# A pool of their own for the exponents, head 0's key scales spread by GpSimd, and the first projection products placed among the attention's last ones

## The chip, the cores and the metric

The kernel runs on one core of one Trainium2 chip. The metric is the time of one execution on the device in microseconds; 2890.35 us is the median of three runs before the change (2888.08 to 2891.64). Five engines take part, each with its own queue of instructions that it works off in order: TensorE (PE), VectorE (DVE), ScalarE (ACT), GpSimd (POOL) and SyncE (SP). Transfers are issued from the queues of SP, POOL and ACT.

## The reference: what is computed

One layer of a perceiver: cross-attention of 512 tokens to 8192 context tokens, then causal self-attention, then a gated feed-forward block with four-bit weights. Each adds to `x`. The change lies in the cross-attention and in the step from it to the self-attention:

```python
q = (layernorm(x) @ Wq + bq)          # 512 x 1024, 16 heads of 64
kv = ctx @ Wkv + bkv                  # 8192 x 2048
q = fq_sym(q / 8, axis=-1)            # quantised to 127 steps, scale per token and head
k = fq_sym(k, axis=-1)                # the same, per key and head
v = fq_sym(v, axis=tokens)            # per column
attn = fq_unsigned(softmax(q @ k.T))  # 255 steps, scale per row
x = x + (attn @ v) @ Wp + bp          # "the projection"
x = x + self_attention(layernorm(x))  # causal, 4 sequences of 128, rotary
x = x + ffn(layernorm(x))             # silu(gate) * up, down, RMS norm
```

## The kernel before, in words

The work has five stages in program order.

1. The queries are computed, then values and keys of all 64 context tiles of 128 tokens (`project`, L336; `join`, L350). A float32 product is done as three products of rounded parts: a high part, a low part scaled up, and a difference (`split_hi` on ACT, `split_lo` on DVE). Keys are quantised (`quantise`), transposed by DMA (`transpose_k`, L565), cast on ACT into `kst` and stored to memory as `k_d` by POOL (`store_k`, L576). The keys' scales are collected for 16 tiles, transposed by TensorE, copied by ACT and stored as `sk_d` (`key_scales`, L595). There are four key chunks `c` of 2048 keys.
2. At the end of that stage, head 0's keys (`load_keys`, L611) and scales (`load_scales`, L620) are loaded on the SP queue. Each of the eight scale tiles `sk` is a DMA that writes one row of 1024 scales to all 128 partitions, 512 KB. For heads 1 to 15 four rows are loaded instead (`load_rows`, L731), and GpSimd broadcasts them over the partitions (`spread_scales`, L737).
3. Attention runs over 64 units (16 heads by 4 query tiles) of 8 steps each, 1024 keys a step. In the loop of L876, step `s` issues the scores of unit `s // 8` (`scores`, L746: two products into PSUM, then one DVE instruction at L766 that multiplies by the scales into `e` and takes the maximum), the exponentials of the unit before (`exponentials`, L789, ACT, 4096 wide, into int16 `a`), transposes of `a` with a lag of 12 steps (`transposes`, L803: by TensorE with an ACT copy of PSUM into `aT`; chunks 1 and 3 by DMA instead, `dma_transposes`, L817), and the products with the values with a lag of 18 steps (`values`, L828). After the last query tile of a head, DVE scales the result into `xo`. Since each queue is worked in order, the order of these calls is the order of work; 18 steps after the last scores only transposes and value products remain.
4. Projection and self-attention. A list of work (`do(step, function)`, L1198 on) is sorted by its step numbers and issued in that order. There are ten parts of 32 steps: part 0 and part 1 are the two halves of the projection by `Wp`. Part 0 uses whole float32 products (`first_step`, L1005) on transposed `xo` (`first_transposes`, L976, a TensorE transpose and ACT copies into `xoT`), so its weights `wp` need no splitting. Part 1 uses `product_step` (L1016), with the parts `x_h`, `x_l`, `x_d` of the input (`first_split`, L985) and `sw_h`, `sw_l`, `sw_d` of the weights. Weights come in pairs of rows, loaded on SP into `w_raw`, which has two buffers (`load_pair`, L953; `split_pair_hi`, `split_pair`). Each part has four pairs. The result is joined to `x1` by DVE (`join_residual`, L1038), after POOL has added the bias row (`add_row`, L973). PSUM accumulators have two buffers a tag.
5. The feed-forward block.

Memory is managed in pools that open and close as a stack on the left or the right side of SBUF. When a pool closes, the next one takes its bytes, and the first writer of the new tile waits for the last reader of the old one. In the kernel before, the exponents `e` are a tag of the pool `at` (L753), opened after `opool` and `at_s`.

Of the kernel before, what the change touches and what calls it, by code (L numbers as in the profile page):

```python
# [46 lines left out]
P = 128  # L47
# [15 lines left out]
LAG_V = NSC + 10  # L63
DMA_KC = (1, 3)
# [20 lines left out]
def tile_perceiver(  # L85
# [111 lines left out]
    nsq = qpool.tile([P, NT, H], F32, name="nsq")  # L197
# [113 lines left out]
    def double_q():  # L311
        nc.vector.tensor_scalar_mul(nsq, sq, -1.0)
        nc.scalar.dma_start(out=qT[D:P, 0:H:2, :], in_=qT[0:D, 0:H:2, :])
        nc.scalar.dma_start(out=qT[0:D, 1:H:2, :], in_=qT[D:P, 1:H:2, :])
# [280 lines left out]
    def key_scales(c):  # L595

        row = pools["k"].tile([P, 2 * P], F32, name="sk_row", tag="sk_row", bufs=1)
        for e in range(2):
            pt = kv_ps.tile([P, P], F32, name="sk_pt", tag="ps")
            nc.tensor.transpose(pt, sks[c].rearrange("p h (i e) -> p e h i", e=2)[:, e], ident)  # L600
            nc.scalar.copy(in_order(row, c)[:, :, e], pt)
# [18 lines left out]
    def load_scales(h, g):  # L620
        c, half = divmod(g, 2)
        nc.sync.dma_start(
            out=tile_of_scales(h, g), in_=sk_d[c][h, ts(half, SC)].partition_broadcast(P)
        )
# [78 lines left out]
    for c in range(NKC - 1):  # L703
        do(at + 0.3, load_keys, 0, c)
        for g in range(2 * c, 2 * c + 2):
            do(at + 0.3, load_scales, 0, g)
# [6 lines left out]
    opool_s = ExitStack()  # L713
    opool = opool_s.enter_context(tc.tile_pool(name="opool", bufs=1))
    xo = [opool.tile([P, NT, 512], F32, name=f"xo{n}", tag=f"x{n}") for n in range(2)]
    both = opool.tile([P, 2, C], F32, name="sv_bp", tag="x2")
    sv, bp = both[:, 0, :], both[:, 1, :]

    with tc.tile_pool(name="at_s", bufs=4) as small, tc.tile_pool(
        name="at", bufs=2  # L720
    ) as at, tc.tile_pool(name="sc_ps", bufs=2, space=PSUM) as sc_ps, tc.tile_pool(
        name="at_ps", bufs=3, space=PSUM
    ) as at_ps:
        vqs = {}
# [6 lines left out]
        def load_rows(h):  # L731

            sks_at[h] = at.tile([P, KC], F32, name=f"sk_row{h}", tag="sk_row", bufs=1)
# [12 lines left out]
        def scores(n, g):  # L746
# [5 lines left out]
            if g % (NSC // NEC) == 0:  # L752
                e = at.tile([P, EC], F32, name="e", tag="e", bufs=3)  # L753
                state[n]["e"].append(e)
# [22 lines left out]
        def maximum(n):  # L777
# [6 lines left out]
                m, m, nsq[:, t, h : h + 1], math.log(255.0), ALU.mult, ALU.add  # L784
# [4 lines left out]
        def exponentials(n, c):  # L789
# [9 lines left out]
                scale=sq[:, t, h : h + 1],  # L799
# [3 lines left out]
        def transposes(n, g):  # L803
# [9 lines left out]
            nc.scalar.copy(aT, pt.bitcast(I32))  # L813
# [48 lines left out]

        load_keys(0, NKC - 1)
        for g in range(NSC - 2, NSC):
            load_scales(0, g)
        load_rows(1)
        nc.sync.dma_start(out=sv, in_=sv_d[0].partition_broadcast(P))
        nc.sync.dma_start(out=bp, in_=xbp.partition_broadcast(P))
# [3 lines left out]
        def at_step(s):  # L872
            return divmod(s, NSC) if 0 <= s < n_steps else None

        with tc.manual_schedule():
            for s in range(n_steps + LAG_V):  # L876
# [25 lines left out]
                if at_step(s - LAG_V):  # L902
                    values(*at_step(s - LAG_V))

# [5 lines left out]
    xq.close()  # L910
    xpool = ctx.enter_context(tc.tile_pool(name="xpool", bufs=1, side="right"))
    x1 = xpool.tile([P, NT, C], F32, name="x1")
    sa_s = ExitStack()

    x3_s = ExitStack()
    x3pool = x3_s.enter_context(tc.tile_pool(name="x3pool", bufs=1, side="right"))
    x3 = [x3pool.tile([P, NT, NC, P], F32R, name=f"x3_{c}") for c in "hld"]
# [6 lines left out]
    sa_ps = sa_ps_s.enter_context(tc.tile_pool(name="sa_ps", bufs=2, space=PSUM))  # L924

# [8 lines left out]
    w_first = {}  # L934
    w3s = {}
    acc = {}
    live = {}

    def load_first(k):
        tag = "qT" if k < 4 else ("kT" if k < 6 else "aT")  # L940
        w = sa_f.tile([P, 512], F32, name=f"wp0_{k}", tag=tag, bufs=4 if k < 4 else 2)
        nc.sync.dma_start(out=w, in_=w_src2[0][:, k, :])
        w_first[k] = w

    def load_x(t):
        nc.sync.dma_start(out=x1[:, t, :], in_=x[ts(t, P), :])
# [37 lines left out]

    def first_split(t):  # L985
        hi, lo, df = (x[:, t] for x in x3)
        split(live["xoT", t], hi, lo, df)
        nc.scalar.mul(lo, lo, UP)
# [16 lines left out]
    def first_step(t, k):  # L1005
        if k == 0:
# [459 lines left out]
```

## Time and profile before

| What | Value |
|---|---|
| Median of three runs | 2890.35 us |
| The profiled execution | 2888.83 us |
| Its span, first to last instruction | 2887.1 us |
| Mean granted TensorE clock | 0.978 |
| PE busy | 2666.1 us (92%) |
| DVE busy | 2411.5 us (84%) |
| ACT busy | 1271.2 us (44%) |
| POOL busy | 444.4 us (15%) |
| Last product of stage 1 starts | 1499.10 us |
| First exponent `e` | 1510.93 us |
| Last `e` starts | 2149.31 us |
| Last product with the values | 2164.22 us, for 0.64 |
| First product of part 1 | 2208.82 us |

Times within the profile are counted from the first instruction. A row of a group gives the line, the engine, the operation, and out<-in by tile names; a bracket gives how long the engine stood idle before and what released it. The clock is the share of full speed that was granted to TensorE.

### The profile page before, as it was taken

The numbers are of one execution on the slowest core, as the hardware profiler recorded it, in microseconds if no ns is written. First come the engines' busy times: TensorE is split into PE (matmuls) and PEld (weight loads), VectorE is DVE, ScalarE is ACT, GpSimd is POOL, SyncE is SP. The second block draws the span as 40 slices with busy tenths as digits, with TensorE's granted clock in tenths as the row PEclk, the third lists the DMA queues.
The fourth block names the chain that finished last, engine by engine and source line by source line (L and its number), as shares of the span: only waits on it lengthen the run. The fifth ranks groups of instructions, "written<-read, shape, count | busy, mean of one in ns | idle before, by whom it ended". The sixth has DMA issues, their size and how long they took to land. (4 is left out here: it accounts for less than half of the span.)

```text
span 2887.1 us, 41022 instructions
## 1 busy us (share of the span) xinstructions
PE 2666.1 (92%) x15480; PEld 2066.9 (72%) x15480; DVE 2411.5 (84%) x3946; ACT 1271.2 (44%) x1409; POOL 444.4 (15%) x596
## 2 busy tenths in 40 slices
PE   8999999999999999999987777787778899799998
PEld 3788888888888888888864555555555777688876
DVE  6899999555799998889769999999986898676674
ACT  4211111111323333333218999999993245333332
POOL 0011111000012222222112233322311000000000
PEclk9999999999999999999998999999999999899999
DMA  5555565222447777777457788878773221122222
GB/s 186 173 195 203 193 214 206 94 98 93 135 133 199 199 183 193 183 193 184 109 154 145 153 164 168 164 162 154 155 132 121 95 70 63 54 92 93 94 90 93
DMA packets 454342, 417.33 MB, mean 145 GB/s; under 512 B 357184, under 2 KB 361856, under 8 KB 454144
## 3 DMA queue, kind: packets, MB, share of 16 engines
q1 hardware_dynamic: 407648, 260.58, 37.1%
q0 software_dynamic: 45440, 153.09, 16.6%
q8 instruction: 121, 1.98, 0.3%
q10 hardware_dynamic: 1056, 1.05, 0.2%
q14 instruction: 77, 0.63, 0.1%
HBM read 224.30 MB, written 104.34 MB: 114 GB/s over the span
## 5 line engine op out<-in xcount | busy, mean ns | idle before, releaser
L342 PE MATMUL kv_a<-w_h,c_h 128*128 128x512 f32 x2048 | 806.4, 394 | 0.0
L342 PE MATMUL kv_b<-w_d,c_d 128*128 128x512 f32 x2048 | 806.0, 394 | 0.3 <-DVE c_d L157 0.3
L342 PE MATMUL kv_a<-w_l,c_l 128*128 128x512 f32 x2048 | 806.0, 394 | 0.2 <-ACT w_l L245 0.2
L766 DVE CUSTOM_DVE_ANT_0 e<-sc,sk 128x1024 f32<-128x1024 f32 x512 | 593.2, 1219 | 16.2 <-DMA k_d<-kst 8.2
L794 ACT ACTIVATE a<-e,m,sq 128x4096 int16<-128x4096 f32 x128 | 487.0, 3805 | 25.0 <-DVE m L783 24.8
L342 PEld LDWEIGHTS kv_a<-w_l,c_l 128*128 128x128 f32 x2048 | 384.8, 188 | 89.6 <-ACT w_l L245 0.6
L342 PEld LDWEIGHTS kv_b<-w_d,c_d 128*128 128x128 f32 x2048 | 384.8, 188 | 89.5 <-DVE c_d L157 0.7
L342 PEld LDWEIGHTS kv_a<-w_h,c_h 128*128 128x128 f32 x2048 | 384.9, 188 | 88.9 <-issue 0.2
L153 ACT ACTIVATE c_h<-c_raw 128x1024 fp32r<-128x1024 f32 x128 | 135.2, 1057 | 414.7 <-PE kv_a L342 405.5
L356 DVE SCALAR_TENSOR_TENSOR f<-kv_a,bkv 128x512 f32<-128x512 f32 x256 | 175.8, 687 | 163.4 <-PE kv_a L342 162.8
L759 PE MATMUL sc<-kt,qT 64*128 64x512 bf16 x1024 | 207.3, 397 | 108.9 <-DVE mx L766 104.6
L581 ACT CAST kst<-kT 128x512 bf16<-128x512 int16 x128 | 89.4, 698 | 310.1 <-DMA kT<-ki 310.0
L809 PE MATMUL a_pt<-ident,a 128*128 128x128 f32 x1024 | 176.9, 298 | 22.7 <-ACT a L794 18.0
L357 DVE SCALAR_TENSOR_TENSOR f<-kv_b,f 128x512 f32<-128x512 f32 x256 | 176.7, 690 | 20.0 <-DVE f L356 1.4
L739 POOL PARTITION_BROADCAST sk<-sk_row x120 | 142.7, 1299 | 317.9 <-DVE mx L766 317.8
L809 PEld LDWEIGHTS a_pt<-ident,a 128*128 128x128 f32 x1024 | 112.9, 146 | 88.6 <-ACT a L794 50.6
L759 PEld LDWEIGHTS <-qT 64*128 64x128 bf16 x1024 | 74.8, 93 | 137.3 <-issue 107.8
L156 DVE TENSOR_TENSOR fw_l<-fw_raw,fw_h 128x1024 fp32r<-128x1024 f32 x64 | 78.3, 1223 | 107.1 <-ACT fw_h L153 107.0
L156 DVE TENSOR_TENSOR c_l<-c_raw,c_h 128x1024 fp32r<-128x1024 f32 x128 | 155.7, 1216 | 6.0 <-ACT c_h L153 5.5
L157 DVE SCALAR_TENSOR_TENSOR c_d<-c_l,c_raw 128x1024 fp32r<-128x1024 f32 x128 | 156.3, 1221 | 2.3
L153 ACT ACTIVATE fw_h<-fw_raw 128x1024 fp32r<-128x1024 f32 x64 | 67.7, 1060 | 179.5 <-PE y_a L1369 75.2
L548 ACT CAST vq<-vi 128x1024 f16<-128x1024 int16 x64 | 66.9, 1046 | 172.2 <-DVE vi L541 123.8
(189 smaller groups left out, 4100.6 us busy)
## 6 DMA issues: line engine op xcount, KB each, us to landing
c_raw<-in_ctxT SPq DMA_DIRECT2D x128, 512.0 KB, 3.8
v_d<-f POOLq DMA_DIRECT2D x64, 512.0 KB, 3.1
vl<-v_d POOLq DMA_DIRECT2D x64, 512.0 KB, 4.2
gu_d<-w_ffn POOLq DMA_DIRECT2D x44, 512.0 KB, 3.2
fw_raw<-gu_d SPq DMA_DIRECT2D x42, 512.0 KB, 3.2
k_d<-kst POOLq DMA_DIRECT2D x128, 128.0 KB, 3.6
vq_d<-vq POOLq DMA_DIRECT2D x32, 512.0 KB, 5.1
kt<-k_d SPq DMA_DIRECT2D x64, 256.0 KB, 3.5
```

The costliest lines, as they stand in the source:

```text
L153: nc.scalar.mul(hi, src, 1.0 - 0.5 / UP)
L156: nc.vector.tensor_tensor(lo, src, hi, ALU.subtract)
L157: nc.vector.scalar_tensor_tensor(df, lo, -1.0 - UP, src, ALU.mult, ALU.add)
L342: nc.tensor.matmul(ps, lhsT=tokens[s][i][:, k, :], rhs=w3[s < KT][k][i][:, ts(n, 512)], start=(k == 0 and i != 1), stop=(k == NC - 1 and i ...
L356: nc.vector.scalar_tensor_tensor(f, a, 1.0 + 1.0 / UP, bias[s < KT][n], ALU.mult, ALU.add)
L357: nc.vector.scalar_tensor_tensor(f, b, -1.0 / UP, f, ALU.mult, ALU.add)
L581: nc.scalar.copy(in_order(kst, c)[:, :, :, u % 2], kTs.pop((u, n)))
L739: nc.gpsimd.partition_broadcast(tile_of_scales(h, g), sks_at[h][32 * c : 32 * c + 1, ts(half, SC)], channels=P)
L759: nc.tensor.matmul(ps[:, ts(i, 512)], lhsT=qT[rows, h, ts(t, P)], rhs=kts[h, g // 2][rows, ts(g % 2, 512)], start=True, stop=True,)
L766: nc.vector.tensor_tensor_reduce(out=state[n]["e"][-1][:, ts(g % (NSC // NEC), SC)], in0=ps, in1=sks_at[h, g], scale=1.0, scalar=LOWEST, o ...
L794: nc.scalar.activation(a, st["e"][c], AF.Exp, bias=st["m"], scale=sq[:, t, h : h + 1], accum_out=sums[h][:, t, c : c + 1],)
L809: nc.tensor.transpose(pt[:, i, :], a[:, at_word + P * i : at_word + P * i + P], ident)
```

## The change

Four things, in the order of the program.

Head 0's scales. `load_scales(c)` now loads two rows of 4 KB of chunk `c` on SP into `sk_half`, and a new `spread_first(c)` broadcasts them by GpSimd. The calls stand at new places, and the `bp` row is no longer loaded here. The PSUM copies of the last chunk's scales move from ACT to DVE. `nsq` goes; `sqs` holds both signs.

The pool. `e` and `sk_row` get a pool `at_e` that is opened first.

The attention's end. For the last two units, DVE takes ACT's PSUM copies into `aT` (of the last unit but one only the steps from 2 on). When all scores have been issued, `open_projection` closes the scores' PSUM pool and the pool of queries and keys, and loads the first weights (two transfers of 1 MB, tile `wp0`) and the first half of `x` (1 MB) on POOL's queue. `first_chunks` transposes tiles 0 and 1 of the finished heads, copied by DVE; then 14 of the 32 products of part 0 (input chunks 0 to 6 of tiles 0 and 1) have new places: eight at the steps `FIRST_AT` after the last scores, six at the head of the list of stage 4.

Part 0 and part 1. `wp0` lies where the difference tile of `x3` comes to lie, so that this tile is written after part 0 (`first_difference`), and tile 0 of part 1 does its difference products last. Tiles 0 and 1 are split and joined at steps 14 to 16; the second half of `x` is loaded at 15.4 on POOL, into bytes that held `xoT` of tiles 0 and 1.

```diff
+FIRST_AT = (5, 6, 7, 14, 15, 17, 17, 17)
...
-            nc.scalar.copy(in_order(row, c)[:, :, e], pt)
+            copy = nc.scalar.copy if c < NKC - 1 else nc.vector.tensor_copy
+            copy(in_order(row, c)[:, :, e], pt)
...
-    def load_scales(h, g):
-        c, half = divmod(g, 2)
-        nc.sync.dma_start(
-            out=tile_of_scales(h, g), in_=sk_d[c][h, ts(half, SC)].partition_broadcast(P)
-        )
+    def load_scales(c):
+
+        if c == 0:
+            sks_at["rows"] = pools["keys"].tile([P, SC], F32, name="sk_half")
+        row = sks_at["rows"]
+        for half in range(2):
+            p = 32 * (2 * (c % 2) + half)
+            nc.sync.dma_start(out=row[p : p + 1, :], in_=sk_d[c][0:1, ts(half, SC)])
+
+    def spread_first(c):
+        for half in range(2):
+            p = 32 * (2 * (c % 2) + half)
+            nc.gpsimd.partition_broadcast(
+                tile_of_scales(0, 2 * c + half), sks_at["rows"][p : p + 1, :], channels=P
+            )
...
-                e = at.tile([P, EC], F32, name="e", tag="e", bufs=3)
+                e = at_e.tile([P, EC], F32, name="e", tag="e", bufs=3)
...
-            nc.scalar.copy(aT, pt.bitcast(I32))
+
+            copy = nc.scalar.copy if n < len(units) - 2 or g < 2 and n < len(units) - 1 else nc.vector.tensor_copy
+            copy(aT, pt.bitcast(I32))
...
+        def open_projection():
+
+            sc_s.close()
...
+            xq.close()
...
+            wp0 = x3pool.tile([P, NC, 512], F32, name="wp0", tag="d")
+            live["third"] = lambda: x3pool.tile([P, NT, NC, P], F32R, name="x3_d", tag="d")
...
+            for t in range(2):
+                live["xoT", t] = live["x1"][:, 2 + t].rearrange("p (c q) -> p c q", q=P)
+            for i in range(2):
+                nc.gpsimd.dma_start(out=wp0[:, ts(i, 4), :], in_=wp0_src[:, ts(i, 4), :])
+            load_x(0)
...
+        meanwhile = {0: [(open_projection,)]}
+        for i, at_s in enumerate((3, 3, 4, 4)):
+            meanwhile.setdefault(at_s, []).append((first_chunks, i // 2, i % 2))
+        early_steps = [(t, k) for t in range(2) for k in range(NC - 1)]
+        for at_s, step in zip(FIRST_AT, early_steps):
+            meanwhile.setdefault(at_s, []).append((first_step, *step))
...
                 if at_step(s - LAG_V):
                     values(*at_step(s - LAG_V))
+                for fn, *args in meanwhile.get(s - n_steps, ()):
+                    fn(*args)
...
-        w3 = w3s[h, k // 2]
         a, b = acc[h, t]
-        for i, ps in enumerate((a, a, b)):
+        steps = [(i, ps, k) for i, ps in enumerate((a, a, b))]
+        if (h, t) == (1, 0):
+            last = [(2, b, k) for k in range(NC)] if k == NC - 1 else []
+            steps = steps[:2] + last
+        for i, ps, k in steps:
...
+        do(-10, last_chunks)
+        for step in early_steps[len(FIRST_AT) :]:
+            do(-9.4, first_step, *step)
+        for n in range(2):
+            do(-10, keep, ("bp", n), load_bias, xbp, n)
+            for t in range(NT):
+                do((-9, 15.5)[t // 2] + 8 * n, lambda t, n: add_row(t, n, rows["bp", n]), t, n)
+        do(15.4, live["load_x"], 1)
...
-                    do(g - 4.5, first_transposes, t)
-                    do(g + 1.5, first_split, t)
+                    if t < 2:
+                        e = 15 + t
+                        do(14.2 + t, first_split, t)
+                    else:
+                        do(-9.5 if t == 2 else g - 4.5, first_transposes, t)
+                        do(g + 1.5, first_split, t)
+                    do(PART + (0.05, 3, 9, 15)[t], first_difference, t)
```

## The prediction

> **What bounds the kernel now.** I first read the busy time by stretches. It splits the run into a projection stage in which TensorE never pauses (up to 1499.5 us), an attention stage in which VectorE is full (489.4 of 500 us between 1600 and 2100), and a last stage in which TensorE is the fullest again. At the two seams nobody is full. In these rows the columns are PE, PE weight load, DVE, ACT, POOL, TensorE clock, DMA share, GB/s.
>
> ```profile
> 1500.00:1520.00 20.00, 5.69 (x19) 1.20 (x20) 11.52 (x20) 2.08 (x5) 7.18 (x13) 0.57 1.02 295
> 1600.00:2100.00 500.00, 394.06 (x4798) 276.90 (x4797) 489.38 (x951) 479.86 (x401) 151.37 (x171) 0.97 0.80 161
> 2150.00:2160.00 10.00, 5.97 (x83) 5.58 (x84) 1.19 (x6) 10.00 (x10) 0.00 (x0) 0.83 0.69 107
> 2160.00:2170.00 10.00, 6.42 (x98) 5.16 (x96) 1.96 (x4) 3.93 (x7) 0.50 (x2) 0.76 0.54 117
> 2170.00:2180.00 10.00, 8.68 (x24) 3.65 (x22) 1.54 (x2) 1.06 (x1) 4.33 (x4) 0.90 1.02 386
> 2180.00:2190.00 10.00, 6.33 (x10) 2.71 (x11) 6.76 (x5) 3.92 (x5) 6.52 (x5) 0.66 0.35 113
> ```
>
> Then VectorE in order of time at the first seam: its last projection work ends at 1502.68, and the first exponent `e` starts 8.25 us later, on a landed store of the key buffer.
>
> ```profile
> 1501.99 0.69 DVE L188 TENSOR_TENSOR ki<-f,rs 128x512 int16<-128x512 f32 x1
> 1510.93 1.22 DVE L766 CUSTOM_DVE_ANT_0 e<-sc,sk 128x1024 f32<-128x1024 f32 x1 [8.25 <-DMA k_d<-kst]
> ```
>
> At the second seam the chain of waits shows what ends last: the last DMA transpose, the first projection weights, then the weights of the next half.
>
> ```profile
> 2159.69 4.49 DMA aT_d<-a
> 2164.22 0.65 PE av L835 x16
> 2164.90 0.44 DVE xo L850
> 2165.36 0.56 DVE xo L858
> 2167.44 0.43 SPq L942
> 2167.91 6.14 DMA wp<-in_xWp
> 2174.07 8.00 DMA w_raw<-in_xWp
> 2182.08 1.06 ACT sw_h L153
> ```
>
> So 44 us lie between the last attention product (2164.86) and the first product of the second projection half (2208.82).
>
> **Part 1, the exponents' pool and the scales of head 0.** The wait of 8.25 us is on memory: `e` lies today on the bytes of `kst`, which the last `k_d` stores read until 1510.9. With a pool opened first it lies on the projection weights, whose last reader is TensorE at 1499.5. What is late next? VectorE now also makes the two small `sk_row` copies (two took ACT 0.43; on DVE the same is assumed), after `ki` at 1502.7, so to about 1503.3; ACT no longer queues them behind a key cast at 1503.60. The first scores, held today to 1504.60 by those copies, run from 1503.6, and `e` starts near 1504.4. Six `e` at their pitch of 1.145 us bring it to 1511.3, where the last key chunk is wanted. Its scales: `sk_d` issued 1503.5, 3.8 us to landing as now, two row loads of 4 KB (about 3 us, as the `sk_row` loads' 3.5), then one broadcast of 1.30: 1512.3. Its keys: `k_d` issued 1504.1 behind `sk_d` on POOL, about 3.5 to landing, `kt` 2.8: 1511.3, scores 0.6 more. So the seventh `e` starts at 1512.4 and the eighth, one broadcast later, at 1513.7; the maximum comes at 1515.0 instead of 1520.45. Saved: 5.5 us. From there everything is as before, moved. On SP eight broadcast loads of 512 KB go, eight row loads come; on POOL eight broadcasts (8 x 1.30 = 10.4 us) come, six of them before 1503 where POOL is idle, and the `vq` loads, behind them, issue about 0.5 us later than now, 13 us ahead of their first use.
>
> A rule against this: the Trainium skill, "SBUF — State Buffer", section "SBUF: two separate sides", says that a VectorE instruction with two SBUF inputs and a GpSimd instruction that reads SBUF hold a shared port in turn, each for its whole length. `ki` (two SBUF inputs) now has a broadcast beside it. The row that is there, `e` during broadcasts in attention, stays at 1.22 us, but one of its inputs is in PSUM. By the rule `e` would begin up to 1.3 us later (1505.7), by the row not at all. As the seventh `e` waits about 1.1 us for its scales anyhow, the rule takes 0.2 off the 5.5, the row nothing; I take nothing and keep 3.5 to 6.7.
>
> **Part 2, the end of attention.** On today's time axis:
>
> ACT loses the two `aT` copies between the last two exponentials (0.95 us), so the last one ends at 2158.6, the last transpose is issued at 2158.7 and lands 4.4 later at 2163.1. The ten copies that DVE takes over or gains (0.69 each as other 128x512 reads of PSUM, 6.9 us) lie in its idle 8.71 us before 2159.70.
>
> The first weights (2 MB) and half of `x` (1 MB) leave SP, where they were issued from 2166.1 on, for POOL, right after the last `e` (2150.5). Four `vq` loads, also 2 MB on POOL, took 1513.5 to 1520.8; so half of the weights land near 2156, all near 2159, `x` near 2161. That is beside the last transposes, and transposes beside such loads land late:
>
> ```profile
> DMA to landing us min/median/max: 4.2/4.4/9.0
> ```
>
> TensorE's queue from 2154.9: two groups of transposes (0.5 each), 7 transposes of finished heads (0.8), three first steps, the products of the last units (0.33 a group), two more first steps. One step is two records; eight take 7.03 us:
>
> ```profile
> 2183.67 6.36 PE L1008 MATMUL acc_a<-wp,xoT 128*128 128x512 f32 x8 [3.96 <-ACT xoT L982]
> 2190.74 7.03 PE L1008 MATMUL acc_a<-wp,xoT 128*128 128x512 f32 x16
> ```
>
> That is 0.88 a step with the full clock (1.6 in the first of these rows, in the half clock). Summed, the last product ends at 2166.8, 1.9 later than now, with five of 32 steps done. Clock: today a pause of 2.79 us (2152.2 to 2155.0) was followed by half clock until about 2158.5. "TensorE: Matmul & The Clock Gate", section "What's actually happening", says that it takes an idle window of about 3.4 us; by that rule the new pause of 1.9 us costs nothing, by the row it could halve the clock again, +1.7 us. The row has the longer pause, so I take 0 and keep 1.7 for the range.
>
> After 2166.8: three steps (to 2169.5), the last chunk's and tile 2's transposes (1.1, to 2170.6), eight steps of tiles 0 and 1 (to 2177.6). Tile 2 then needs an accumulator, which `join_residual` of tile 0 frees. And that has moved behind a wait. ACT, in order: copies (2171.3), `sw_h` of weight pair 0 and 1 (2173.4), then `sw_h` of pair 2, which has only two raw buffers and so waits for DVE's split of pair 0 (`sw_l`, `sw_d`, to 2174.9) and a new load of 3.6 us:
>
> ```profile
> L960 SPq DMA_DIRECT2D w_raw<-in_xWp x4: 368/373/385, 2174.1 to 2193.8; - x4
> ...
> DMA to landing us min/median/max: 3.5/3.6/8.6
> ```
>
> so to 2178.7. Behind it: `x_h` of tile 0 (2180.8), on DVE `x_l` (2182.1), then the join (2182.8). TensorE idles 2177.6 to 2182.9 and starts tile 2 in the half clock, which lasted some 4.5 us at 2183.67: two and a half steps in 4.4, five and a half in 4.8, transposes of tile 3 0.9: 2193.0. Tile 3 needs its own copies, on ACT behind `x_l` scaling of tile 2, ready 2192.9; its 7.0 us end at 2200.0. Now the second half starts, 8.8 us earlier than 2208.82.
>
> Its tile 0 runs the `a` products (16 x 0.233 = 3.7, to 2203.7) and then needs the difference tile, which can only be written when the first weights, whose bytes it takes, are read (2200.0), and which on DVE stands behind two weight pairs (to 2204.4 at best) and takes 1.2: a stall of 2.0. Later the bias rows of tiles 2 and 3, added on POOL near 2191 to 2196 after a load that waits for tile 1's split, run beside DVE's splits; today that doubled one:
>
> ```profile
> 2183.17 2.22 DVE L156 TENSOR_TENSOR sw_l<-w_raw,sw_h 128x1024 fp32r<-128x1024 f32 x1 [11.59 <-ACT sw_h L153]
> ```
>
> One such doubling, half of it on the path: 0.5. Left: 8.8 - 2.0 - 0.5 = 6.3. From there to 2510 TensorE is busy 237.8 of 260 us and the order is unchanged, so the lead passes through.
>
> **Sum.** 5.5 + 6.3 = 11.8. The profiled execution took 2888.83 (its span 2887.1, 1.7 around it): 2877.0. The median of the runs shown is 1.5 above it, so 2878.5.
>
> **Rivals.** (A) TensorE is fed throughout: tile 2 doesn't wait for the join. 27 steps (23.8) and 2.2 of transposes after 2166.8 start the second half at 2192.8, 16 earlier; less 1 for the difference: 15 + 5.5, so 2870. For it: DVE idles at 2169 to 2172. Against it: the third raw load can't be issued before `sw_d`. (B) Seam two gives nothing: the 3 MB beside the transposes make the last one land after 9.0 instead of 4.4 (2167.7), products end 2168.5 or later, TensorE is cold (1.7), the chain behind moves with both and a raw load takes 6 instead of 3.6: about 5.8 of the 6.3. Left 6.0: 2884. (C) Slower: a first step stands in TensorE's queue ahead of the last head's products and waits for weights on POOL's queue. Each microsecond of landing after 2157.4 delays all behind it one for one. At 2169.2 the gain of both seams is gone, from 2175.0 on it is slower by over 0.2% (5.8 us); at 2180 it would be 2901. Against it: no 512 KB load there took over 6.7 us. (D) The pool doesn't free the first `e`, since scales or keys still come at 1511: then part 1 gives 1 and the whole 7.3: 2883.
>
> **How the numbers follow.** Main case 0.62, A 0.13, B 0.12, C 0.06, D 0.07. No change that a measurement of this kernel can tell is within 0.2%, 5.8 us, so 2884.6 to 2896.1. Faster: the main case but for 0.02, A, D and half of B, 0.86; same: that 0.02 and the other half of B, 0.08; slower: C, 0.06. Main case alone: 2874 to 2883 (part 1 3.5 to 6.7, part 2 4 to 10). Eight in ten: 2868 to 2886, which takes in A, B and D.
>
> **What would show it.** First `e` 1.7 us after `ki` instead of 8.25, and a short wait before the seventh, on POOL's `sk`. The weights' load issued within 1 us of the last score. The last transpose landing 4 to 6 us after its issue. TensorE idle some 5 us before tile 2, with ACT's `sw_h` waiting for `w_raw`. A stall of 2 us before the first `acc_b`. The prediction is wrong if TensorE doesn't idle there (A), if first steps wait for `wp0` (C), or if the attention's pitch changes.

## The result, and the profile after

The changed kernel takes 2878.83 us (median of 8 runs, 2874.83 to 2884.0), the kernel before 2890.68 beside it: a ratio of 0.9961, 95% interval 0.9947 to 0.9974, 7 to 15 us faster. A second set gave 2879.45 against 2889.67, 0.9958 (0.9945 to 0.9970). The prediction was 2878.5.

The first profile of the changed kernel has a span of 2882.1 us, one of its longer executions; a second has 2878.6. I also took a second profile of the kernel before, 2887.7. Cut at five events that the timeline shows in all four (the end of the last `kv` product, the first unit's maximum `m`, the start of the last `e`, the end of the last attention product, the start of the fourth normalised tile `xn` of the projection):

| us | before | before, second | after | after, second |
|---|---|---|---|---|
| to the end of the last `kv` product | 1499.50 | 1498.93 | 1500.04 | 1500.05 |
| to the first maximum | 20.71 | 20.48 | 14.97 | 14.97 |
| to the last `e` | 629.10 | 629.93 | 629.16 | 628.79 |
| to the last attention product | 15.55 | 15.53 | 20.17 | 19.74 |
| to the fourth `xn` | 82.39 | 82.56 | 77.44 | 74.73 |
| to the end | 639.80 | 640.32 | 640.34 | 640.31 |

The first seam is 5.5 to 5.7 us shorter in both profiles. The second (fourth and fifth row of times together) was 97.9 to 98.1 and is 97.6 or 94.5: the attention's last product comes 4.2 to 4.6 later, what follows it 5 to 8 us sooner.

The busy time by stretches of the first profile after, with the columns as before:

```profile
1500.00:1520.00 20.00, 8.28 (x29) 1.63 (x27) 18.91 (x36) 5.58 (x4) 12.01 (x17) 0.62 0.55 172
1600.00:2100.00 500.00, 393.81 (x4796) 276.58 (x4795) 489.37 (x951) 478.76 (x398) 152.58 (x172) 0.97 0.83 161
2150.00:2160.00 10.00, 9.09 (x93) 7.11 (x93) 4.21 (x8) 3.56 (x2) 0.50 (x2) 0.84 1.08 352
2160.00:2170.00 10.00, 9.11 (x73) 5.38 (x74) 0.97 (x3) 2.62 (x6) 4.68 (x4) 1.00 0.81 221
2170.00:2180.00 10.00, 4.96 (x12) 1.90 (x10) 6.36 (x6) 2.95 (x4) 0.27 (x1) 0.86 0.33 105
2180.00:2190.00 10.00, 9.50 (x24) 4.43 (x24) 7.00 (x8) 5.27 (x7) 1.77 (x2) 0.80 0.41 141
```

At the first seam VectorE is now busy 18.91 of 20 us (11.52 before); the attention is unchanged; TensorE is nearly full to 2170 and then has its hole between 2170 and 2180. VectorE at the first seam, by time, from its last work on keys to the first exponent (the short rows between are left out):

```profile
1503.25 1.28 DVE L190 TENSOR_TENSOR ki<-f,rs 128x512 int16<-128x512 f32 x1
1504.45 0.47 DVE L602 COPY sk_row<-sk_pt 128x128 f32<-128x128 f32 x2
1505.74 1.22 DVE L787 CUSTOM_DVE_ANT_0 e<-sc,sk 128x1024 f32<-128x1024 f32 x1 [0.81 <-PE sc L780]
```

The wait of 8.25 us is 0.81 now, and it is on TensorE's scores, not on a store. The chain of waits at the second seam:

```profile
2153.57 2.98 SPq L845
2156.66 3.87 SPq L845
2160.88 4.29 DMA row<-in_xbp
2165.32 2.50 POOL x L1042 x2
2167.82 0.33 ACT xoT L1050
2168.77 1.08 ACT sw_h L155
2169.87 1.49 DVE sw_l L158
2171.39 1.24 DVE sw_d L159
2172.68 3.84 DMA w_raw<-in_xWp
2176.54 1.06 ACT sw_h L155
2177.60 0.95 ACT x_h L155
2178.57 1.24 DVE x_l L1064
```

The last transposes are still first in it (L845, on SP's queue until 2160.5). From `sw_h` on, where projection weights and one raw load of 8 us stood, there is now an interplay of ScalarE, VectorE and the third raw load. Between the two, this chain goes by a bias row and GpSimd, the chain of the second profile by TensorE's products; in both, `sw_h` starts 4.43 us after the last attention product. And rows of TensorE's own around its two pauses, 5.54 us before tile 2 and 4.21 us before the first `acc_b`:

```profile
2167.93 7.03 PE L941 MATMUL acc_a<-wp,x 128*128 128x512 f32 x16
2180.50 5.38 PE L941 MATMUL acc_a<-wp,xoT 128*128 128x512 f32 x8 [5.54 <-issue]
2186.60 10.69 PE L941 MATMUL acc_a<-wp,xoT 128*128 128x512 f32 x24
2205.22 3.78 PE L1100 MATMUL acc_b<-sw_d,x_d 128*128 128x512 f32 x8 [4.21 <-DVE x_d L1072]
```

### The profile page after: what moved, and what is told of

Its sections match the earlier page's. It is cut to its first block, busy times and chain, and to the rows that moved or that the text cites. A ratio compares the mean times of both kernels' runs of the same rounds, so it can differ in the third digit from the quotient of the medians.

```text
span 2882.1 us, 41034 instructions
## 1 busy us (share of the span) xinstructions
PE 2666.1 (93%) x15480; PEld 2067.8 (72%) x15480; DVE 2418.6 (84%) x3959; ACT 1266.1 (44%) x1399; POOL 454.6 (16%) x608
## 4 chain that ended last, share of the span: by engine, by line
PE 71%; DVE 20%; issue 4%; POOL 2%; ACT 1%; DMA 1%; SPq 0%; DVEq 0%; ACTq 0%; POOLq 0%
PE kv_a L342 33%; PE kv_b L342 16%; DVE e L787 13%; PE acc_a L1100 3%; PE y_a L1454 3%; PE gate_a L165 3%; PE up_a L165 3%; POOL sk L760 2%; PE acc_b L1100 2%; PE y_b L1454 1%; PE gate_b L165 1%; PE up_b L165 1%; PE q_ps L292 1%; PE a_pt L830 1%; PE sc L780 1%
## 5 line engine op out<-in xcount | busy, mean ns | idle before, releaser
L815 ACT ACTIVATE a<-e,m,sqs 128x4096 int16<-128x4096 f32 x128 | 486.9, 3804 | 25.2 <-DVE m L804 24.8
```

The source lines that it names most:

```text
L815: nc.scalar.activation(a, st["e"][c], AF.Exp, bias=st["m"], scale=sqs[:, 0, t, h : h + 1], accum_out=sums[h][:, t, c : c + 1],)
```

## The experiments

Times beside a run of the kernel before come from four further sets on the chip, so kernels are compared by their ratio to the kernel before of their own set. "Theory" is the prediction's reasoning, amended as the runs came in.

### The changed kernel and the kernel before once more

No edit in either.

> The changed kernel as it is, once more, for a second profile beside the kernels of this set. The one profile of it so far took 5.0 us less than the profile of before (span 2882.1 against 2887.1), while the medians differ by 11.85. Theory: the profiled execution was one of the slow ones of its kernel, since each stall of the projection's start (5.54 us before tile 2, 4.21 us before the first acc_b) varies with the landing of loads; a second profile shows the same two stalls, together 6 to 10 us, and a time of 2875 to 2884. Rival: the stalls of the first profile are an accident, together under 3 us here.

> The kernel before, unchanged, for a second profile of it. In the profiles so far the attention (first to last e) took 638.4 us with 8 windows of half clock of 3.4 us each, 643.1 with 13 and 647.5 with 15 of them, two of which lasted 6.8 (from 45 us after the first e on). Theory: how many there are changes from execution to execution of one kernel, so this profile may have another number than before's 8, and its attention lasts 638.4 plus about 1 us for each window more. Rival (the number belongs to the kernel): 8 windows and 638.4 us again.

The changed kernel: 2879.45 us (ratio 0.9958), span 2878.6. Its two pauses are 5.46 and 2.77 us: both are there again, and the second varies. The kernel before: 2889.52, its attention with 9 windows of half clock lasted 639.2 us from first to last `e`. The first profile has 8 such windows and 638.4 us. So the number changes from execution to execution, and the attention's length with it (more on it at the end).

### Each part alone

Part 2 alone is the changed kernel with this undone (and with it the place of `sk_row` and the last chunk's scale copies, which go back to ScalarE):

```diff
-    with tc.tile_pool(name="at_e", bufs=1) as at_e, tc.tile_pool(
+    with tc.tile_pool(
...
-                e = at_e.tile([P, EC], F32, name="e", tag="e", bufs=3)
+                e = at.tile([P, EC], F32, name="e", tag="e", bufs=3)
...
-        spread_first(NKC - 1)
+        for g in range(NSC - 2, NSC):
+            load_scales(0, g)
```

> The changed kernel with part 1 undone: exponents back in the pool that they shared, head 0's scales by broadcasting DMAs, the last two scale copies on ScalarE. Theory: the first e starts again about 8 us after ki, the maximum of the first unit 5 to 5.5 us later than in the changed kernel, and the time is 5 to 5.5 us more than the changed kernel's (about 2884); part 2 alone is worth 5 to 7 of the 11.85 us. Rival (part 2 gives nothing, as the first profile reads: its lead is 6.5 us at the first product of the second tile of the second half, 5.1 of them from the first seam): within 2 us of the kernel before (2889 to 2891).

It took 2888.90, ratio 0.9997 (0.9989 to 1.0006): no difference. The rival had the number, but not for its reason. In the profile the stretch from the last `e` to the fourth `xn` is 94.51 us, 3.4 to 3.6 less than before. At the first seam, the maximum comes 23.27 after the last `kv` product, 2.6 to 2.8 later than before (the first `e` waits 10.74 us for a load of `sk`), which takes most of it back; why this layout is worse than the one before I did not follow up.

The pool alone is the kernel before with three lines changed:

```diff
-    with tc.tile_pool(name="at_s", bufs=4) as small, tc.tile_pool(
+    with tc.tile_pool(name="at_e", bufs=1) as at_e, tc.tile_pool(name="at_s", bufs=4) as small, tc.tile_pool(
...
-            sks_at[h] = at.tile([P, KC], F32, name=f"sk_row{h}", tag="sk_row", bufs=1)
+            sks_at[h] = at_e.tile([P, KC], F32, name=f"sk_row{h}", tag="sk_row")
...
-                e = at.tile([P, EC], F32, name="e", tag="e", bufs=3)
+                e = at_e.tile([P, EC], F32, name="e", tag="e", bufs=3)
```

> The kernel before with the exponents (and the rows of scales) in a pool of their own, opened first, and nothing else of the change: scales of head 0 by broadcasting DMAs, scale copies on ScalarE, attention's end as before. Theory (the wait of 8.25 us was on memory alone): the first e starts 1.7 to 3 us after ki, the seventh waits for its keys and scales near 1512.5, the maximum of the first unit comes 4.5 to 5.5 us earlier against the end of the last ki than before, and the time is 4 to 6 us less (near 2885). Rival (the broadcasts or row loads are what counts, without them the scales come as late as the memory did): under 1.5 us gained.

It took 2882.48, ratio 0.9966 (0.9954 to 0.9979): about 9 us, of the 10 to 12 of the whole change, and more than the theory allowed. VectorE in its first seam:

```profile
1505.59 1.23 DVE L766 CUSTOM_DVE_ANT_0 e<-sc,sk 128x1024 f32<-128x1024 f32 x1 [3.24 <-PE sc L759]
1514.52 1.23 DVE L766 CUSTOM_DVE_ANT_0 e<-sc,sk 128x1024 f32<-128x1024 f32 x1 [1.97 <-PE sc L759]
```

The first `e` waits 3.24 us for scores, the seventh 1.97 for scores whose keys are late; the maximum comes 17.76 after the last `kv` product, 2.7 to 3.0 us sooner than before. The rest I had not seen coming: the second seam shrank too, to 94.57 us, with not one instruction of it changed. SP's queue shows where. First its waits in the kernel before, near the last transposes (queue, for what, us in total, times, longest):

```profile
SPq L942 <- DVE xo L858: 4.0, 1, 4.0
```

then the same queue's issues with the pool alone:

```profile
2149.47 11.58 SPq L822 DMA_TRANSPOSE aT_d<-a  x3
2161.40 1.12 SPq L942 DMA_DIRECT2D wp<-in_xWp  x2
```

The first weights waited 4.0 us for the last `xo` and were issued at 2166.1; now nothing holds them behind the last transpose, and they are issued at 2161.4. Only places in memory differ between the two kernels, so this was a wait on memory as well. (By the code, `xo` at L858 is also the last to read a small tile of the pool `at_s`, and the pool of the weights opens where `at_s` closed; that these bytes are the reason is likely, but the record has no addresses.) The two parts' gains at the second seam do not add: 94.57 by the pool alone, 94.51 by part 2 alone, 94.47 or 97.61 with both.

The spread alone undone in the changed kernel:

```diff
-        spread_first(NKC - 1)
+        for g in range(NSC - 2, NSC):
+            load_scales(0, g)
...
-            copy = nc.scalar.copy if c < NKC - 1 else nc.vector.tensor_copy
-            copy(in_order(row, c)[:, :, e], pt)
+            nc.scalar.copy(in_order(row, c)[:, :, e], pt)
```

> The changed kernel with only the way of head 0's scales undone: broadcasting DMAs of 512 KB each as before, and the last two scale copies on ScalarE; the pool and the new end of attention stay. Theory (with memory out of the way, the last scales and keys set the seventh and eighth e): the first unit's maximum comes 17.5 to 18 us after the end of the projection's products, as in pool_alone (17.76), not 14.97 as in the changed kernel, and the time is 2 to 3.5 us more, near 2882. Rival (the broadcasts on GpSimd cost at the shared port what they save, ki took 1.28 us beside them instead of 0.69): within 1 us of the changed kernel's 2879.

It took 2881.08, ratio 0.9973 (0.9961 to 0.9984). The maximum comes 18.72 us after the last product, so the broadcasts and the two scale copies together are worth 2.8 us (against the pool alone) to 3.8 us (against the changed kernel) at the seam. By the ratios the time is 3.5 to 4.3 us longer than the changed kernel's, with intervals that overlap. That speaks for the theory, not the rival. What the broadcasts are worth without the copies is not shown: the first `e` is already 1.9 us later than in the changed kernel.

### TensorE's pause before tile 2

Both joins of tiles 0 and 1 ahead of the splits, and tile 3's transposes early; then with the difference tile ahead of two weight pairs too:

```diff
+                    e = 13.9 + t if t < 2 else e
                     do(e + 0.2, join_residual, h, t, n)
...
-                        do(-9.5 if t == 2 else g - 4.5, first_transposes, t)
+                        do(-9.5 if t == 2 else -9.3, first_transposes, t)
...
-                    do(PART + (0.05, 3, 9, 15)[t], first_difference, t)
+                    do(PART + (-0.8, 3, 9, 15)[t], first_difference, t)
...
-                    do(at + 0.5, split_pair, h, kp)
+                    do(31.3 if (h, kp) == (2, 0) else at + 0.5, split_pair, h, kp)
```

> The changed kernel with the joins of tiles 0 and 1 ahead of the splits of xoT (on VectorE behind the second weight pair, with nothing of ScalarE's third sw_h before them), and tile 3's transposes ahead of tile 0's last step. Theory (TensorE's pause before tile 2 is the join queued behind the sw_h that waits for its w_raw): the pause of 5.54 us shrinks to about 1, the second half starts 5 to 6 us earlier (near 2191 on the axis of the first profile), and the stall before the first acc_b grows to about 7, as the difference tile still stands behind two weight pairs, of which the last raw load comes about 3.5 us earlier: 3 to 4 us gained, near 2875. Rival (the pause is the transposed chunks or the projection weights): the pause stays over 4 us and the time stays at 2879.

> As joins_early, and the first difference tile ahead of the two weight pairs of the third part in VectorE's order. Theory (the 4.21 us before the first acc_b are the difference tile behind those pairs, whose last raw load was issued late): both stalls go, the first acc_b follows the a products within 1 us, and the time is 10 to 12 us under the changed kernel's, near 2867.5. Rival (VectorE is the bound there, so what is taken from one wait is given to the next: joins, statistics and splits come later): 3 to 5 us gained, near 2875, with new pauses of TensorE between 2200 and 2250.

They took 2884.99 (0.9983) and 2883.72 (0.9978): both are slower than the changed kernel, and the pause is 5.48 us still. The experiment was badly made. ScalarE in the second one:

```profile
2172.96 1.07 ACT L1050 COPY xoT<-pt 128x512 f32<-128x512 f32 x2 [4.83 <-PE pt L1049]
2173.92 2.02 ACT L155 ACTIVATE sw_h<-w_raw 128x1024 fp32r<-128x1024 f32 x2
```

Tile 3's copies stand ahead of the first `sw_h` in ScalarE's queue, and wait 4.83 us for transposes that stand behind six early steps in TensorE's. The first `sw_h` starts at 2173.92 instead of 2167.98. It tells nothing of the join, but it shows what 6 us on the first `sw_h` cost: 2.9 to 5.6 at the fourth `xn` (80.31 us after the last attention product; 74.73 and 77.44 in the changed kernel). Put right (the transposes at -9.45, ahead of the steps, tile 1's last step at 14.05 and both joins at 14.1):

> joins_diff put right: there tile 3's transposes stood behind TensorE's early steps and its two copies ahead of ScalarE's first sw_h, which began 5.9 us late (2173.92 against 2167.98) and moved all of VectorE's splits. Here those transposes stand ahead of the early steps, and both joins follow tile 0's and 1's last steps at once. Theory (pause before tile 2 = join behind sw_h; stall before acc_b = difference behind two weight pairs): the first sw_h 1 us later than in the changed kernel, TensorE's pause before tile 2 about 1 us instead of 5.5, the second half starts near 2190 instead of 2196, the first acc_b follows the a products within 1 us, and the first normalised block comes 7 to 10 us earlier than in the second profile of the changed kernel; time near 2870. Rival (VectorE is full from the first sw_l on): both stalls move and the first normalised block comes within 3 us of the changed kernel's; time 2877 to 2881.

```profile
2177.25 14.00 PE L941 MATMUL acc_a<-wp,xoT 128*128 128x512 f32 x32 [0.40 <-DVE x L1117]
2195.66 0.77 PE L1100 MATMUL acc_a<-sw_h,x_h 128*128 128x512 f32 x1 [4.41 <-DVE x L1117]
```

The pause before tile 2 is 0.40 us: the join's place was its cause. TensorE has all four tiles done 26.0 us after the last attention product instead of 32.9, and then waits 4.41 us for the next join. The fourth `xn` comes 75.80 after that product (74.73 and 77.44 in the changed kernel), the time 2878.34 (0.9956): nothing gained. The rival was right. TensorE does not set the end of this stretch: after those 4.41 us it waits 1.96 us more for VectorE's next join and 1.12 us for a difference tile.

Without the eight early steps:

```diff
-FIRST_AT = (5, 6, 7, 14, 15, 17, 17, 17)
+FIRST_AT = ()
```

> The changed kernel without its eight early steps between the last attention products: all fourteen first steps stand behind the attention, weights and x are loaded as in the changed kernel. As the prediction reckons (TensorE sets the end there), five steps of 0.88 us go behind the last attention product, 4.4 us, and that product comes up to 2.5 us earlier: 2 to 4 us slower, near 2882. Rival (VectorE's and ScalarE's splits set the end, and they start from the transposes behind the last attention product): the last product comes 1.5 to 2.5 us earlier after the last exponential than the 10.4 to 10.8 us of the changed kernel, the splits with it, and the time is the same or up to 2 us less, 2877 to 2879.

```profile
2160.42 1.03 PE L858 MATMUL av<-vq,aT_d 128*128 128x64 f16 x16 [4.91 <-DMA aT_d<-a]
2166.61 14.97 PE L941 MATMUL acc_a<-wp,x 128*128 128x512 f32 x32
```

It took 2878.98, ratio 0.9959: the same as with them. The pause of 5.5 us is gone, since the steps that moved back fill it, and the second half starts as late as with them. The last attention product comes only 0.4 to 0.8 us sooner after the last exponential than with the steps (9.98 against 10.35 and 10.77): TensorE stands 4.91 us, and the products that follow run at half clock (1.03 for sixteen, 0.63 otherwise). So the rival had the time, and its reason only in part. The work named in the change's title, first products between the last ones, is worth nothing measurable here.

### The loads beside the last transposes

```diff
-            load_x(0)
...
+        do(-9.95, live["load_x"], 0, nc.sync)
```

> The changed kernel with the first half of x (1 MB) not on GpSimd's queue beside the last DMA transposes but on SP's queue behind them; the projection weights (2 MB) stay. Theory (the last transpose lands late, 6.9 us after the last exponential against 4.6 before, since 3 MB of loads share the DMA engines with it): it lands about 1 us earlier, the last attention product with it, and the time is 0.5 to 1.5 us under the changed kernel's. Rival (the transposes are late for their own issue, or the weights alone do it): no earlier landing, and the join of tile 0, whose bias row needs x, comes no earlier: within 1 us of the changed kernel.

The chain of waits after the last exponential, in this kernel:

```profile
2156.74 2.03 SPq L845
2158.88 2.87 SPq L845
...
2164.13 8.44 DMA w_raw<-in_xWp
```

In the changed kernel the same rows are 2.98 and 3.87 us. The first row is only what is left of its transpose when the exponential ends: whole, it held SP's queue for 6.75 us there and 5.80 here, the last one 3.87 and 2.87. The tile's rows before and after give shortest, median and longest time on the queue in ns:

```profile
L822 SPq DMA_TRANSPOSE aT_d<-a x9: 1689/1918/3217, 2120.2 to 2159.7; - x9
L845 SPq DMA_TRANSPOSE aT_d<-a x8: 1317/1863/6747, 2120.0 to 2156.7; - x8
```

With 1 MB less beside them the transposes are done 5.0 us after the last exponential, not 7.0. And it gains nothing (2879.92, ratio 0.9965, 0.9953 to 0.9977), since the raw weights, now behind `x` on SP, take 8.44 us: the first `sw_l` starts 8.26 us after the last attention product, not 5.53. The contention is shown; its 2 us were given to the next load.

### ScalarE's queue

Two `sw_h` moved, nothing else:

```diff
-                    do(at - 2.5, split_pair_hi, h, kp)
+                    do({(1, 2): 15.3, (1, 3): 17.4}.get((h, kp), at - 2.5), split_pair_hi, h, kp)
```

> The changed kernel with two operations moved on ScalarE alone: sw_h of the third weight pair of the second half behind the splits of xoT of tiles 0 and 1, sw_h of the fourth ahead of tile 2's. Theory (ScalarE stands 5.7 us at that sw_h, which waits for its w_raw, and x_h, x_l and the join stand behind it): ScalarE no longer waits there, TensorE's pause before tile 2 falls from 5.5 to 2 or 3 us, the steps end 1 to 3 us earlier after the last attention product than the 32.9 us of the two profiles of the changed kernel. For the time: 1 to 3 us gained (near 2877) if TensorE sets the end of this stretch, within 1 us of 2879 if the chain of splits between ScalarE and VectorE does, as joins_diff_2 suggests.

It took 2874.76, ratio 0.9943 (0.9930 to 0.9956): 4 to 5 us under the changed kernel by the ratios, more than either expectation, though the intervals overlap. ScalarE, first in the changed kernel's first profile:

```profile
2168.77 2.02 ACT L155 ACTIVATE sw_h<-w_raw 128x1024 fp32r<-128x1024 f32 x2
2176.54 1.06 ACT L155 ACTIVATE sw_h<-w_raw 128x1024 fp32r<-128x1024 f32 x1 [5.75 <-DMA w_raw<-in_xWp]
2177.50 1.04 ACT L155 ACTIVATE x_h<-x 128x1024 fp32r<-128x1024 f32 x1
```

and in this one:

```profile
2172.59 2.01 ACT L155 ACTIVATE sw_h<-w_raw 128x1024 fp32r<-128x1024 f32 x2
2174.49 1.05 ACT L155 ACTIVATE x_h<-x 128x1024 fp32r<-128x1024 f32 x1
2179.93 1.06 ACT L1065 ACTIVATE x_l<-x_l 128x1024 fp32r<-128x1024 f32 x1 [4.38 <-DVE x_l L1064]
```

`x_h` follows the second `sw_h` at once. TensorE's pause is 1.82 us, and the fourth `xn` comes 68.53 after the last attention product (74.73 and 77.44). The busy time from about the first `sw_l` to the fourth `xn`, in the changed kernel's second profile, in joins_diff_2 and in this kernel:

```profile
2169.00:2238.00 69.00, 54.75 (x197) 35.48 (x195) 55.05 (x70) 24.49 (x33) 8.51 (x6) 0.93 0.25 84
```

```profile
2171.70:2241.00 69.30, 55.00 (x188) 35.73 (x187) 55.91 (x71) 23.72 (x30) 7.82 (x5) 0.92 0.25 84
```

```profile
2173.70:2236.70 63.00, 51.57 (x196) 33.35 (x194) 56.93 (x72) 24.57 (x32) 8.67 (x6) 1.00 0.28 92
```

VectorE's work (third pair of numbers) is 55 to 57 us in all three; what differs is its idle time, 13.95, 13.39 and 6.07. In joins_diff_2 it waits at `x_l` and `sw_l` for ScalarE, whose `sw_h` still stands waiting for its raw load. The granted clock is 1.00 here and 0.93 and 0.92 there; what share of the gain that is, is not shown.

All of it together, with the late bias rows on VectorE:

```diff
+                late = n == 1 and t > 1
...
+                    47 if late else (-9, 15.5)[t // 2] + 8 * n,
...
+                    nc.vector if late else nc.gpsimd,
```

> joins_diff_2 and hi_late together, and the bias rows of the second half's tiles 2 and 3 added on VectorE behind the first normalised block, not on GpSimd beside the splits. Theory (from TensorE's 32 steps on, VectorE and ScalarE pass splits to and fro and set the end: in joins_diff_2 VectorE is idle 6.3 us before the first acc_b waiting for ScalarE, and loses 2.2 to 3 us in operations that GpSimd's additions hold up): these idle times fall under 3 us and the held-up operations from three to one or two, the first normalised block comes 4 to 5 us earlier than in joins_diff_2 (44.6 us after the last attention product there), near 40; time near 2874. Rival (only the sum of VectorE's work counts): within 1.5 us of joins_diff_2, 2877 to 2880.

It took 2874.68, ratio 0.9945 (0.9932 to 0.9958): near the number expected, but no better than hi_late alone. The first `xn` comes 39.99 after the last attention product, as expected (hi_late: 40.00), the fourth 70.04. The first `acc_b` follows the `a` products at once. The copies of tile 3, ahead of ScalarE's first `sw_h`, cost 1 us at the start; what joins and difference give, they give to pauses that did not set the end. hi_late is the version to keep: one line.

## Why the prediction was right, and where it was not

**Part 1 (5.5): right.** 5.74 in the first pair of profiles, 5.51 in the second, by two errors that cancel. `ki` beside a broadcast took 1.28 us, not 0.69, and without broadcasts, in no_spread, 0.69 again: the Trainium skill's rule of the shared port ("SBUF — State Buffer", section "SBUF: two separate sides"), which I had weighed and left out, was right for an operation with two inputs in SBUF, where the `e` row was no measure. `sk` just before it took 0.82 beside the broadcast and 0.17 without, so the two lost 1.2 us; the rule had been put at up to 1.3. The first `e` started 5.70 us after the last `kv` product, not 4.9. And the wait of 1.1 before the seventh, which I had foreseen, was not there. Most of it was a slip: the terms for its scales add up to 1511.6, not 1512.3, and those for its keys to 1510.4, not 1511.3, which leaves 0.3 us, and the later start covers that. The maximum came 14.97 us after the last `kv` product; 15.5 was predicted.

**Part 2 (6.3): 0.3 in the first profile, 3.6 in the second.** Set from the start of the last `e`:

| us after the last `e` | before | predicted | after | after, second |
|---|---|---|---|---|
| last attention product ends | 15.55 | 17.5 | 20.17 | 19.74 |
| first product of the second half | 59.5 | 50.7 | 52.6 | 52.0 |
| fourth `xn` | 97.9 | 91.6 | 97.6 | 94.5 |

- *The transposes* were reckoned at 4.4 us, with up to 9.0 possible, and the delay sat elsewhere: not in the last one, but in the one ahead of it, which held SP's queue for 6.75 us (6.44). The last was issued 12.5 us (12.2 in the second profile) after the last `e`, where 9.4 was expected, and left the queue 3.87 (3.72) later. That is the 2.2 to 2.7 us of the first row. x_late shows one of the three MB as the cause of about 2.0.
- *TensorE's queue* was right. From the last attention product to the pause 10.6 us (10.8 predicted), the pause 5.54 (5.3), from its end to the end of the steps 16.8 (17.1). Its cause, `sw_h` waiting for `w_raw` with the join behind it, is shown twice: by hi_late, and by joins_diff_2.
- *The stall before the first `acc_b`* was 4.21 and 2.77, not 2.0, and the half clock behind it was not in the sum: the eight `acc_b` products took 3.78 and 2.88 us, where the full clock gives 0.233 each, 1.87. The doubled VectorE operations are two of 2.36 and 2.17 us in the first profile, one of 2.18 in the second, beside GpSimd's bias rows; 0.5 was allowed. (The prediction says that one was doubled before; it was two there as well, of 2.22 and 2.17.)
- *Summed*, these terms are the whole shortfall. The first `acc_b` came 61.0 and 59.1 us after the last `e` where 56.4 was predicted, and its eight products took 1.9 and 1.0 longer; less the 0.5 set aside that is 6.0 and 3.2, and at the fourth `xn` 6.0 and 2.9 are missing. From the end of those products on, the lead did pass through, within 0.6 us.
- What the sum had wrong in kind is its carrier. It started from TensorE's start of the second half and took 2.0 off. But from the first `sw_l` on, splits pass between ScalarE and VectorE, and the first `acc_b` waits for their last, the difference tile. joins_diff_2 gave TensorE 6.8 us and the end nothing; no_early took the early steps away and the end stayed.

**The sum** (11.8) met the medians (11.85 and 10.2) and is larger than what the traces add up to, so that it fits to 0.3 us is luck. The first pair of profiles is 4.94 apart, the second 9.16: 5.51 at the first seam, 3.62 at the second, 0.03 elsewhere. The remaining 1 to 3 us are inside the interval of the ratio and stay open. The mean granted clock of the runs is 0.981 after and 0.978 before, but the half clock at the first seam alone is shorter (27.3 and 20.5 us after, 34.1 and 30.7 before), and in the attention the four profiles hardly differ (8 and 8 half-clock windows after, 8 and 9 before).

**The rivals.** A (TensorE fed throughout) was built as joins_diff_2 and gives nothing: it had the same wrong engine. Of B, the late transposes came, by 2.2 to 2.7 us; the slow raw load did not (3.84 and 3.62 us for the third, where 3.6 was reckoned and B had 6), until x_late made one. C's mechanism appears in three profiles: the first early step waits for `wp`, 1.39 us in the second profile after, 1.52 in hi_late, 1.57 in all_reordered. It costs nothing visible: the last attention product comes no later there. D did not come: the pool frees the first `e`.

**What I did not see** is that the pool would act at the second seam. The chain of before has `xo` directly ahead of SP's L942, and I read it as the order of SP's queue; the view of waits says that L942 waited 4.0 us for `xo`, a tile it does not read. With the pool alone that wait is gone, and three lines give about four fifths of the whole change by the medians (6 to 13 us by the interval).

## What to carry to other kernels

When a load waits for an engine whose result it does not use, it may well wait for memory, as twice here: look for such rows before moving work, since a pool's place can end several of them at once. Before filling an engine's pause, ask which engines the work behind it passes between; here TensorE's pause was a symptom, and a further gain lay in one instruction at the head of ScalarE's queue that waited for a load. A transfer moved ahead to where it seems free can slow what it now runs beside, so reckon that delay too.

## What the hardware showed unexpectedly

The granted clock in the records is half for stretches of 3.41 us or a multiple (but for one that the trace's end cuts). Fourteen profiles of the kernels above have 8 to 18 such pieces in the attention (those that begin from 14 us after the first maximum to the last `e`), and the time from that maximum to the last `e` follows their number: 8 pieces 628.8 to 629.2 us, 9 629.9 to 630.0, 11 631.8 to 632.0, 13 633.8, 18 638.2; a line through all is 621.7 us plus 0.92 for each, with a correlation of 0.998. VectorE is full there, and TensorE has spare time on average, and still each piece costs 0.9 us: VectorE idles 0.81 to 0.87 us for each piece, within it and the 3.41 us behind it, and 0.03 in other stretches of 3.41 us. One piece in the first profile after, with the stretches around it, then TensorE's pause ahead of it and VectorE's wait in it:

```profile
1607.08:1610.49 3.41, 1.85 (x24) 1.31 (x24) 3.34 (x9) 3.41 (x5) 0.00 (x0) 1.00 1.08 300
1610.49:1613.90 3.41, 3.41 (x32) 2.28 (x31) 2.75 (x7) 3.41 (x3) 0.00 (x0) 0.50 0.80 153
1613.90:1617.32 3.42, 3.22 (x45) 2.33 (x43) 3.35 (x7) 1.63 (x3) 0.00 (x0) 1.00 0.74 139
```

```profile
1608.10 0.39 PE L858 MATMUL av<-vq,aT 128*128 128x64 f16 x8 [1.35 <-DVE xo L873]
1613.74 1.22 DVE L787 CUSTOM_DVE_ANT_0 e<-sc,sk 128x1024 f32<-128x1024 f32 x1 [0.66 <-PE sc L780]
```

What sets the number can be read from the same traces. Within a profile's attention all pieces begin on one grid of 3.41 us, and TensorE pauses about 1.35 us after each head but the last, waiting for VectorE's `xo`. Of these 210 pauses, the 108 that begin in the last 0.4 or the first 0.9 us of a grid window are each followed by a half-clock piece; the 102 that begin at 1.1 to 3.0 us are followed by none. All but two of the other pieces begin 10.24 us, three windows, after another one. So the number follows from where the heads fall on the grid, and that differs between executions.

The kernel before and the one with most pieces (part 2 alone), over the same 600 us:

```profile
1540.00:2140.00 600.00, 471.72 (x5766) 331.40 (x5762) 588.53 (x1143) 577.47 (x484) 184.08 (x204) 0.98 0.80 158
```

```profile
1540.00:2140.00 600.00, 477.40 (x5709) 334.39 (x5705) 582.46 (x1127) 570.13 (x476) 184.07 (x204) 0.95 0.79 157
```

The clock of 0.95 instead of 0.98 goes with 6 us less of VectorE's time and 16 instructions fewer in the same window. Runs of one kernel differ with it: in 68 runs of the kernel before, whose mean clock is 0.974 to 0.981, 0.001 of clock goes with 1.4 us (correlation -0.79).

The pause of 1.9 us for which the prediction weighed a cold start, soon after the last `e`, was 2.00 us (to 2149.83) in the first profile after, and half clock followed from 2149.8 to 2153.2; the same pause of 1.99 to 2.00 us in the second profile, in hi_late and in no_early was followed by the full clock. By the rule quoted in the prediction neither this pause nor the 1.35 us ones would halve the clock; here the measurement decides, and the length of a pause alone does not tell. Its cost was small at most: the last attention product came 0.4 us later in the first profile than in the second.
